# Moving half of the loads of filter taps from ScalarE's queue to GpSimd's, spreading the other half between loads of x, and reordering the filter steps of a graph network kernel

## The chip, the cores and the metric

The kernel runs on one core of one Trainium2 chip. The metric is the device time of one execution in microseconds (us), median of the runs. Executions of one kernel agree within a few tenths of a per cent here (0.6% at most, in e6_stores_scalar); every run that is compared below is in the fast state. The profiler's span of a run is some 2 us shorter than the time of the same run.

## The reference

The input x is (64, 256, 256): 64 graphs of 256 nodes with 256 channels. What matters is the convolution with 17 taps:

```python
h = relu(layernorm(x))                          # per node
xc = transpose(h, (0, 2, 1))
c = relu(bn1(conv1d(xc, conv1_w, pad=0)))       # 256x256, one tap
c = bn2(conv1d(c, conv2_w, pad=8))              # 256x256, 17 taps
x_conv = transpose(relu(c + xc), (0, 2, 1))
# ... messages over exp(-dist) * adj, then a GRU cell of x_conv, messages and h
return x + gru(...)
```

All is float32.

## The kernel before

The 17-tap convolution is done with transforms of 16 bins, so in the opening the kernel must turn `conv2_w` (the *taps*, 4.4 MB) into filters at the transform's points. This is one small matmul per group of 7 input channels, pass and half: 3 passes times 19 groups = 57 *filter steps*. Each step makes a PSUM tile, ScalarE copies it to an `fo` buffer, and a DMA stores it to a tensor in DRAM, from which the products of the batches load weights `wb`.

```python
KG = P // TAPS                  # 7 channels a group: 7 * 17 = 119 partitions
NG = -(-P // KG)                # 19 groups
taps = stage.tile([KG * TAPS, NG, DC, D], FP, name="taps")

def load_taps(dc, a, b, eng):   # dc: which half of the input channels
    eng.dma_start(out=taps[:, a:b, dc, :],
                  in_=c2_wT[dc * P + a * KG:dc * P + b * KG].rearrange("(g k) t o -> (k t) g o", k=KG))
...                             # (the points of the three passes, on ScalarE's queue)
for h in range(3):
    for dc in range(DC):
        load_taps(dc, h * (NG - 1) // 3, (h + 1) * (NG - 1) // 3, nc.scalar if dc else nc.sync)
for dc in range(DC):            # the rows of the last, smaller group
    last = c2_wT[dc * P + (NG - 1) * KG:(dc + 1) * P]
    nc.sync.dma_start(out=taps[:last.shape[0] * TAPS, NG - 1, dc, :], in_=last.rearrange("k t o -> (k t) o"))
...
def transpose_h(i):             # TensorE transposes x, ScalarE copies to HT
    for dc in range(DC):
        p = aux()
        ...
        nc.scalar.activation(HT[i][:, dc, :], p, AF.Relu)
    if i + 2 < B // G:
        load_x(i + 2, nc.scalar if i < 2 else nc.sync)
...
def filters(m, g, eng):         # one filter step
    p = acc()                   # five PSUM buffers
    for dc in range(DC):
        mm(...)                 # points[m] x taps[:, g, dc]
    t = stage.tile([P, W], FP, name="fo", bufs=6)
    nc.scalar.copy(t[:size * kinds], p[:size * kinds])
    eng.dma_start(out=filt[m][...], in_=t[:size * kinds])
```

The schedule of the opening has four *rounds* (transposes of x, conv1, four filter steps) and then the other filter steps. In their midst the first nine `wb` loads are issued on SyncE's queue:

```python
steps = [(m, g) for m in range(len(PASSES)) for g in range(NG)]
transpose_h(0)
norm(1)
w_msg = ...                     # loads of w_msg and the first adj on SyncE's queue
load_adj(0, nc.sync)
for j in range(PB):             # four rounds
    if j > 0: transpose_h(j)
    if 0 < j < PB - 1: norm(j + 1)
    conv1(j)
    run(split_steps(j))
    for m, n in steps[j * 4:(j + 1) * 4]:
        filters(m, n, nc.sync)
...
for j, (m, n) in enumerate(steps[PB * 4:]):
    filters(m, n, nc.gpsimd if j % 2 else nc.sync)
    if j + PB * 4 == 2 * NG - 10:
        for n in range(3):
            for kind in range(3):
                load_kind(0, n, kind)
```

An engine's program runs in order: what stands behind a waiting instruction or a DMA that can't yet be issued waits too. ScalarE's first copy, for example, stood behind 16.48 us of issuing here, though its input was done at 12.87 us.

Of the kernel before, what the change touches and what calls it, by code (L numbers as in the profile page):

```python
# [13 lines left out]
FP = mybir.dt.float32  # L14
U16 = mybir.dt.uint16
AF = mybir.ActivationFunctionType
# [264 lines left out]
def filter_points(bins, taps):  # L281


    cols = []
    for n in bins:
        z = [(ROOTS[n] if n < 15 else 1.0) ** (taps - 1 - t) for t in range(taps)]
        if n < 15:
            cols += [[v.real for v in z], [v.imag - v.real for v in z], [v.real + v.imag for v in z]]
        else:
            cols += [[1.0] * taps, [(-1.0) ** (taps - 1 - t) for t in range(taps)]]  # L290
    return np.array(cols, np.float64).T
# [10 lines left out]
def kernel(  # L302
# [26 lines left out]
    nc = tc.nc  # L329
    P = 128  # L330
    B, N, D = x.shape
    G = 2
    GB = 8
    PB = GB // G
    NB = B // GB
    DC = D // P
    MC = N // P
    W = G * N
    TAPS = c2_wT.shape[1]
# [9 lines left out]
    const = ctx.enter_context(tc.tile_pool(name="const", bufs=1))  # L349
    work = ctx.enter_context(tc.tile_pool(name="work", bufs=1))  # L350
    stage_ctx = ExitStack()
    stage = stage_ctx.enter_context(tc.tile_pool(name="stage", bufs=1))
# [16 lines left out]
    def chunk(t, g, c):  # L369
        return t[:, g * N + c * P:g * N + (c + 1) * P]  # L370
# [4 lines left out]
    def load_rows(t, src, i, eng):  # L375
        for g in range(G):
            eng.dma_start(out=row_tile(t, g), in_=rows(src, G * i + g))

    def load_x(i, eng=nc.sync):
        X[i] = work.tile([P, G * MC, D], FP, name="x", bufs=2)  # L380
        load_rows(X[i], x, i, eng)
# [23 lines left out]
    def load_adj(i, eng=nc.gpsimd):  # L405
        if i >= B // G:
            return
        if i < BY_DMA:
            ADJ[i] = work.tile([P, G * MC, N], FP, name="adj")
            load_rows(ADJ[i], adj, i, eng)  # L410
            return
        ADJH[i] = late.tile([P, 2 * MC, W], U16, name="adjh")
        for q in range(2 * MC):
            eng.dma_start(out=ADJH[i][:, q], in_=ADJD[i][:, q])
# [26 lines left out]
    neg_half = const.tile([P, G * MC], FP)  # L441
    nc.gpsimd.memset(neg_half, -0.5)

    pace = Pace()

    def mm(p, w, v, columns, **kw):
# [3 lines left out]
    def transpose(p, v):  # L450
        nc.tensor.transpose(p, v, ident)  # L451
        pace.tensor(P / 2)
# [6 lines left out]
    def norm_steps(i):  # L459

        if i >= B // G:
            return [], []
        t = {}

        def stats(j):
            if j == 0:
                t["st"] = work.tile([P, G * MC, 6], FP, name="st")
                t["mv"] = work.tile([P, G * MC, 2], FP, name="mv")
                t["rstd"] = work.tile([P, G * MC], FP, name="rstd")
            nc.vector.bn_stats(t["st"][:, j, :], X[i][:, j, :])  # L470

        def aggregate_stats():
            for j in range(G * MC):
                nc.vector.bn_aggr(t["mv"][:, j, :], t["st"][:, j, :])
            nc.vector.tensor_scalar(t["rstd"], t["mv"][:, :, 1], LN_EPS, None, ALU.add)  # L475
            nc.gpsimd.tensor_tensor(t["rstd"], t["rstd"], neg_half, ALU.pow)  # L476

        def scale(j):
            nc.vector.tensor_scalar(X[i][:, j, :], X[i][:, j, :], t["mv"][:, j, 0:1], t["rstd"][:, j:j + 1],
                                    ALU.subtract, ALU.mult)  # L480

        R = range(G * MC)
        return ([(D, lambda j=j: stats(j)) for j in R] + [(W, aggregate_stats)],
                [(D, lambda j=j: scale(j)) for j in R])

    def run(steps):
        for n, call in steps:
            pace.vector(n)
            call()

    def norm(i):
        a, b = norm_steps(i)
        run(a)
        pace.vector(0, pace.dve + 1.4)
        run(b)
# [3 lines left out]
    def vec(src, name, eng=nc.gpsimd):  # L499
        k = src.shape[0] // P  # L500
        t = const.tile([P, k], FP, name=name)
        eng.dma_start(out=t, in_=src.rearrange("(k p) -> p k", p=P))
        return t

    def bn_vecs(params, name, eng=nc.gpsimd):
        return [vec(a, f"{name}_{s}", eng) for a, s in zip(params, "gbmv")]

    def fold_bn(params, name, factor=1.0):
        g, b, m, v = params
        scale = const.tile([P, DC], FP, name=f"{name}_scale")  # L510
        shift = const.tile([P, DC], FP, name=f"{name}_shift")
        nc.vector.tensor_scalar(scale, v, BN_EPS, None, ALU.add)
        nc.gpsimd.tensor_tensor(scale, scale, neg_half[:, :DC], ALU.pow)
        nc.vector.tensor_mul(scale, scale, g)
        nc.vector.tensor_mul(shift, m, scale)
        nc.vector.tensor_sub(shift, b, shift)
        if factor != 1.0:
            nc.vector.tensor_scalar(scale, scale, factor, None, ALU.mult)
        return scale, shift

    w_c1 = const.tile([P, DC, D], FP)
    nc.scalar.dma_start(out=w_c1, in_=c1_wT.rearrange("(k p) o -> p k o", p=P))
    s1, h1_shift = fold_bn(bn_vecs(bn1, "bn1", nc.scalar), "bn1")


    KG = P // TAPS
    NG = -(-P // KG)
    taps = stage.tile([KG * TAPS, NG, DC, D], FP, name="taps")

    def load_taps(dc, a, b, eng):  # L530
        eng.dma_start(out=taps[:, a:b, dc, :],
                      in_=c2_wT[dc * P + a * KG:dc * P + b * KG].rearrange("(g k) t o -> (k t) g o", k=KG))

    PASSES = [range(0, 6), range(6, 12), range(12, 16)]
    points = []
    for n, bins in enumerate(PASSES):
        f = filter_points(bins, TAPS)
        m = np.zeros((KG, TAPS, KG, f.shape[1]), np.float32)
        for k in range(KG):
            m[k, :, k] = f  # L540
        t = stage.tile([KG * TAPS, KG * f.shape[1]], FP, name=f"points{n}")
        nc.scalar.dma_start(out=t, in_=nc.inline_tensor(m.reshape(KG * TAPS, -1), name=f"points{n}").ap())
        points.append(t)
    for h in range(3):
        for dc in range(DC):
            load_taps(dc, h * (NG - 1) // 3, (h + 1) * (NG - 1) // 3, nc.scalar if dc else nc.sync)
    for dc in range(DC):
        last = c2_wT[dc * P + (NG - 1) * KG:(dc + 1) * P]
        nc.sync.dma_start(out=taps[:last.shape[0] * TAPS, NG - 1, dc, :], in_=last.rearrange("k t o -> (k t) o"))


    Z = const.tile([P, 1 + MC, G * MC, Q], FP, name="z")
# [12 lines left out]
    def aux():  # L565
        return psum.tile([P, W], FP, name="aux", bufs=3)
# [5 lines left out]
    def transpose_h(i):  # L572
        if i >= B // G:
            return
        HT[i] = work.tile([P, DC, W], FP, name="hT", bufs=6)
        for dc in range(DC):
            p = aux()
            for j in range(G * MC):
                transpose(chunk(p, j // MC, j % MC), X[i][:, j, dc * P:(dc + 1) * P])
            nc.scalar.activation(HT[i][:, dc, :], p, AF.Relu)  # L580
        if i + 2 < B // G:
            load_x(i + 2, nc.scalar if i < 2 else nc.sync)



# [44 lines left out]
    def load_kind(b, n, kind):  # L630
        b, n = b + n // BINS, n % BINS
        if b < NB and (n < BINS - 1 or kind < 2):
            WB[b, n, kind] = work.tile([P, DC, D], FP, name="wb", bufs=9)
            m = n // len(PASSES[0])
            nc.sync.dma_start(out=WB[b, n, kind], in_=filt[m][:, 3 * (n - PASSES[m][0]) + kind])
# [209 lines left out]

    w_ih = const.tile([P, 2 * DC, 3 * D], FP)
    w_hh = const.tile([P, DC, 3 * D], FP)
    steps = [(m, g) for m in range(len(PASSES)) for g in range(NG)]
    transpose_h(0)
    norm(1)  # L850

    w_msg = const.tile([P, DC, D + SE], FP)
    nc.sync.dma_start(out=w_msg[:, :, :D], in_=msg_wT.rearrange("(k p) o -> p k o", p=P))
    nc.gpsimd.dma_start(out=w_msg[:, :, D:], in_=se_wT.rearrange("(k p) s -> p k s", p=P))
    b_msg = const.tile([P, D + SE], FP)
    for t, v in ((b_msg[:, :D], msg_b), (b_msg[:, D:], se_b)):
        nc.gpsimd.dma_start(out=t, in_=bass.AP(tensor=v.tensor, offset=v.offset, ap=[[0, P], [1, v.shape[0]]]))
    load_adj(0, nc.sync)
    bn2 = bn_vecs(bn2, "bn2")
    b_ih, b_hh = vec(ih_b, "b_ih"), vec(hh_b, "b_hh")  # L860
    for j in range(PB):
        if j > 0:
            transpose_h(j)
        if 0 < j < PB - 1:
            norm(j + 1)
        conv1(j)
# [3 lines that stand above are left out]
# [5 lines left out]
    forward()  # L875
    for j, (m, n) in enumerate(steps[PB * 4:]):
        filters(m, n, nc.gpsimd if j % 2 else nc.sync)
        if j + PB * 4 == 2 * NG - 10:
            for n in range(3):
                for kind in range(3):  # L880
                    load_kind(0, n, kind)
# [5 lines left out]
    for b in range(NB):  # L887
        i = b * PB
# [158 lines left out]
```

## Time and profile before

| | before |
|---|---|
| time, median of three runs | 1900.42 us |
| span of the profiled run | 1895.5 us |
| TensorE busy, whole span | 96% |
| TensorE busy, first 111.5 us | 75.8 us |
| first message matmul (end of the opening) | 111.51 us |

The page cuts the span into 40 slices and gives busy shares in tenths. The timeline merges neighbouring instructions of one kind: its columns are the start in us, the length in us, engine, line, operation, output and inputs, count, and in brackets how long the engine was idle before it and what ended that. The lines that carry the argument stand in the prediction.

### The profile page before, as it was taken

Reading aid. Unit: us, or ns where it says so; the run is one execution under the profiler, and the core shown is the slowest. Engines: PE = TensorE matmul, PEld = TensorE weight load, DVE = VectorE, ACT = ScalarE, POOL = GpSimd, SP = SyncE. Lnnn points to the kernel's source line nnn. Section 1 sums busy time; section 2 is a strip of 40 time slices with the busy share of each in tenths; the row PEclk is TensorE's granted clock in tenths of the full one; section 3 lists DMA queues with packets and bytes.
Section 4 is the critical chain, followed back from the end, with each engine's and each line's share of the span. In section 5 each row is a group of like instructions: output and inputs, shape, how many; then the busy total and the mean of one; then the engine's idle time right before and its main releaser. Section 6 shows DMA issues by size and latency. Waiting matters only on the chain.

```text
span 1895.5 us, 21978 instructions
## 1 busy us (share of the span) xinstructions
PE 1827.6 (96%) x7708; PEld 1136.6 (60%) x7708; DVE 1393.1 (73%) x2667; ACT 639.4 (34%) x1338; POOL 208.2 (11%) x324
## 2 busy tenths in 40 slices
PE   3999999999999999999999999999999999999997
PEld 2677445865549554694458755495546944586543
DVE  2888648996499945998379964999559983798522
ACT  1534322243313443244232433134432352224311
POOL 2110110110111010111101001101101111010000
PEclk9999999999999999999999999999999999999999
DMA  5777331762318431482316613274313923073010
GB/s 161 253 237 216 91 87 36 195 176 57 85 48 244 107 93 52 112 239 56 89 34 191 182 54 82 54 237 114 90 55 106 239 62 78 23 186 104 2 43 23
DMA packets 180215, 217.63 MB, mean 115 GB/s; under 512 B 86146, under 2 KB 105858, under 8 KB 180105
## 3 DMA queue, kind: packets, MB, share of 16 engines
q1 hardware_dynamic: 145228, 156.03, 28.8%
q0 software_dynamic: 30432, 56.53, 12.7%
q10 hardware_dynamic: 4445, 3.67, 0.6%
q8 instruction: 61, 1.00, 0.2%
q14 instruction: 49, 0.40, 0.1%
HBM read 156.54 MB, written 44.30 MB: 106 GB/s over the span
## 4 chain that ended last, share of the span: by engine, by line
PE 82%; DVE 8%; DMA 4%; issue 3%; ACT 2%; POOL 1%; POOLq 0%; DVEq 0%; ACTq 0%
PE acc L447 70%; PE aux L447 8%; PE aux L451 3%; DMA taps<-in_c_wT_dram 1%; DVE Yv L59 1%; PE aux L736 1%; DVE e L743 1%; DVE Yv L62 1%; DMA x<-in_x_dram 1%; DVE T L65 1%; DVE Yv L65 1%; DVE V L65 1%; DMA wb<-filt 1%; DVE msg L708 1%; DVE T L62 0%
## 5 line engine op out<-in xcount | busy, mean ns | idle before, releaser
L447 PE MATMUL acc<-hT,w_hh 128*128 128x512 f32 x768 | 353.9, 597 | 1.9 <-ACT h L593 1.9
L447 PE MATMUL acc<-xnm,w_ih 128*128 128x512 f32 x768 | 353.0, 594 | 0.0
L447 PE MATMUL acc<-Yv,w_ih 128*128 128x512 f32 x768 | 341.1, 593 | 9.5 <-ACT Yv L696 9.5
L447 PEld LDWEIGHTS acc<-Yv,w_ih 128*128 128x128 f32 x768 | 145.2, 190 | 196.3 <-issue 177.2
L447 PEld LDWEIGHTS acc<-xnm,w_ih 128*128 128x128 f32 x768 | 145.6, 190 | 183.3 <-issue 181.3
L447 PEld LDWEIGHTS acc<-hT,w_hh 128*128 128x128 f32 x768 | 143.5, 191 | 169.5 <-issue 161.4
L797 ACT ACTIVATE tr<-acc,b_rz 128x512 f32<-128x512 f32 x64 | 44.0, 687 | 540.8 <-PE acc L447 540.8
L799 DVE SCALAR_TENSOR_TENSOR gn<-tr,gn 128x512 f32<-128x512 f32 x64 | 44.2, 690 | 207.7 <-ACT tr L797 207.7
L825 POOL DMA_DIRECT2D out_dram<-y x64 | 39.2, 617 | 886.4 <-DVE y L824 885.0
L447 PE MATMUL acc<-hT,w_c 128*128 128x512 f32 x256 | 117.9, 604 | 15.2 <-ACT hT L580 15.2
L447 PE MATMUL acc<-U,wb 128*128 128x128 f32 x1024 | 124.6, 276 | 0.5 <-DMA wb<-filt 0.5
L447 PE MATMUL acc<-V,wb 128*128 128x128 f32 x1024 | 124.8, 275 | 0.0
L447 PEld LDWEIGHTS acc<-U,wb 128*128 128x128 f32 x1024 | 120.5, 192 | 4.3 <-DVE Yv L59 2.3
L59 DVE SCALAR_TENSOR_TENSOR V<-T,V 128x256 f32<-128x256 f32 (+2 forms) x224 | 121.5, 606 | 0.3
L447 PEld LDWEIGHTS acc<-V,wb 128*128 128x128 f32 x1024 | 119.5, 192 | 0.0
L447 PE MATMUL aux<-e,msg 128*128 128x256 f32 x464 | 104.9, 379 | 0.0
L447 PEld LDWEIGHTS aux<-e,msg 128*128 128x128 f32 x464 | 86.1, 190 | 11.4 <-issue 1.0
L476 POOL TENSOR_TENSOR rstd<-rstd,neg_half 128x4 f32<-128x4 f32 x32 | 36.3, 1135 | 502.0 <-DVE rstd L475 502.0
L824 DVE TENSOR_TENSOR y<-aux,y 128x512 f32<-128x512 f32 x64 | 41.1, 683 | 68.4 <-PE aux L451 68.4
L447 PE MATMUL aux<-w_msg,hT 128*128 128x259 f32 x384 | 89.4, 381 | 0.0
L65 DVE TENSOR_TENSOR V<-h 128x512 f32<-128x512 f32 x64 | 43.8, 684 | 60.8 <-ACT h L593 60.8
L447 PEld LDWEIGHTS acc<-hT,w_c 128*128 128x128 f32 x256 | 49.2, 194 | 65.2 <-issue 45.1
(141 smaller groups left out, 2727.6 us busy)
## 6 DMA issues: line engine op xcount, KB each, us to landing
wb<-filt SPq DMA_DIRECT2D x376, 256.0 KB
y<-in_x_dram POOLq DMA_DIRECT2D x64, 256.0 KB, 5.7
out_dram<-y POOLq DMA_DIRECT2D x64, 256.0 KB, 5.1
x<-in_x_dram SPq DMA_DIRECT2D x60, 256.0 KB
halves_d<-halves SPq DMA_DIRECT2D x116, 128.0 KB
adjh<-halves_d POOLq DMA_DIRECT2D x116, 128.0 KB, 5.5
filt<-fo SPq DMA_DIRECT2D x26, 252.0 KB
filt<-fo POOLq DMA_DIRECT2D x10, 252.0 KB, 5.6
```

Of the source, the lines that this page charges most:

```text
L59: return self.step(out, lambda: self.v.scalar_tensor_tensor(out, x, s, y, op0=ALU.mult, op1=ALU.add))
L62: return self.step(out, lambda: self.v.tensor_add(out, x, y))
L65: return self.step(out, lambda: self.v.tensor_sub(out, x, y))
L447: nc.tensor.matmul(p, w, v, **kw)
L451: nc.tensor.transpose(p, v, ident)
L476: nc.gpsimd.tensor_tensor(t["rstd"], t["rstd"], neg_half, ALU.pow)
L708: nc.vector.tensor_add(MSG[i][:, g, c, :], p[:, :D + SE], b_msg)
L736: nc.tensor.matmul(p[:, :N], ZT[rows_q, :P], ZT[rows_q, P:], start=True, stop=True)
L797: nc.scalar.activation(tr, pr, AF.Tanh, bias=b_rz[:, dc:dc + 1], scale=0.5)
L799: nc.vector.scalar_tensor_tensor(gn, tr, 1.0, gn, op0=ALU.add, op1=ALU.mult)
L824: nc.vector.tensor_add(row_tile(Y[i], g), p, row_tile(Y[i], g))
L825: nc.gpsimd.dma_start(out=rows(out, G * i + g), in_=row_tile(Y[i], g))
```

## The change

The intent: ScalarE shall not issue loads of taps, so that it can copy the first transposes at once. GpSimd gets the loads of one half of the channels (all of them at the start), SyncE those of the other in thirds, each behind a load of x. Filter steps now take the first third of the groups through all passes first, so that few taps are needed early. A dummy activation loads ScalarE's table before it is needed. The first `wb` loads move from step 28 to step 40.

```diff
+    def load_last_taps(dc, eng):
+        last = c2_wT[dc * P + (NG - 1) * KG:(dc + 1) * P]
+        eng.dma_start(out=taps[:last.shape[0] * TAPS, NG - 1, dc, :], in_=last.rearrange("k t o -> (k t) o"))
+    THIRDS = [(h * (NG - 1) // 3, (h + 1) * (NG - 1) // 3) for h in range(3)]
+    load_taps(0, *THIRDS[0], nc.sync)          # ahead of norm(0)
+    for t in THIRDS:
+        load_taps(1, *t, nc.gpsimd)
+    load_last_taps(1, nc.gpsimd)
...
+    nc.scalar.activation(const.tile([P, 1], FP, name="unused"), neg_half[:, :1], AF.Relu)
...
-    for h in range(3):
-        for dc in range(DC):
-            load_taps(dc, h * (NG - 1) // 3, (h + 1) * (NG - 1) // 3, nc.scalar if dc else nc.sync)
-    (and the last rows of both halves on nc.sync)
...
-            load_x(i + 2, nc.scalar if i < 2 else nc.sync)
+            load_x(i + 2)
...
-    steps = [(m, g) for m in range(len(PASSES)) for g in range(NG)]
+    FIRST = THIRDS[0][1]
+    steps = [(m, g) for g in range(FIRST) for m in range(len(PASSES))]
+    steps += [(m, g) for m in range(len(PASSES)) for g in range(FIRST, NG)]
     transpose_h(0)
+    load_taps(0, *THIRDS[1], nc.sync)
...                                            # in round j == 1, behind the third load of x:
+            load_taps(0, *THIRDS[2], nc.sync)
+            load_last_taps(0, nc.sync)
+            nc.sync.dma_start(out=w_msg[:, :, :D], ...)
+            load_adj(0, nc.sync)
...
-        if j + PB * 4 == 2 * NG - 10:
+        if (m, n) == (1, NG - 4):
```

More of the change, by code (lines that the diff above doesn't have):

```diff
@@ L442, with load_taps @@
     nc.gpsimd.memset(neg_half, -0.5)
+    KG = P // TAPS
+    NG = -(-P // KG)
+    taps = stage.tile([KG * TAPS, NG, DC, D], FP, name="taps")
+    def load_taps(dc, a, b, eng):
+        eng.dma_start(out=taps[:, a:b, dc, :],
+                      in_=c2_wT[dc * P + a * KG:dc * P + b * KG].rearrange("(g k) t o -> (k t) g o", k=KG))
+    def load_last_taps(dc, eng):
[6 more added lines that the diff above has]
+    load_last_taps(1, nc.gpsimd)
     pace = Pace()
@@ L522 @@
     nc.scalar.dma_start(out=w_c1, in_=c1_wT.rearrange("(k p) o -> p k o", p=P))
-    s1, h1_shift = fold_bn(bn_vecs(bn1, "bn1", nc.scalar), "bn1")
-    KG = P // TAPS
-    NG = -(-P // KG)
-    taps = stage.tile([KG * TAPS, NG, DC, D], FP, name="taps")
-    def load_taps(dc, a, b, eng):
-        eng.dma_start(out=taps[:, a:b, dc, :],
-                      in_=c2_wT[dc * P + a * KG:dc * P + b * KG].rearrange("(g k) t o -> (k t) g o", k=KG))
+    bn1 = bn_vecs(bn1, "bn1", nc.scalar)
+    nc.scalar.activation(const.tile([P, 1], FP, name="unused"), neg_half[:, :1], AF.Relu)
+    s1, h1_shift = fold_bn(bn1, "bn1")
     PASSES = [range(0, 6), range(6, 12), range(12, 16)]
@@ L543 @@
         points.append(t)
-    for h in range(3):
-        for dc in range(DC):
-            load_taps(dc, h * (NG - 1) // 3, (h + 1) * (NG - 1) // 3, nc.scalar if dc else nc.sync)
-    for dc in range(DC):
-        last = c2_wT[dc * P + (NG - 1) * KG:(dc + 1) * P]
-        nc.sync.dma_start(out=taps[:last.shape[0] * TAPS, NG - 1, dc, :], in_=last.rearrange("k t o -> (k t) o"))
     Z = const.tile([P, 1 + MC, G * MC, Q], FP, name="z")
@@ L847 @@
     w_hh = const.tile([P, DC, 3 * D], FP)
-    steps = [(m, g) for m in range(len(PASSES)) for g in range(NG)]
+    FIRST = THIRDS[0][1]
+    steps = [(m, g) for g in range(FIRST) for m in range(len(PASSES))]
+    steps += [(m, g) for m in range(len(PASSES)) for g in range(FIRST, NG)]
     transpose_h(0)
+    load_taps(0, *THIRDS[1], nc.sync)
     norm(1)
     w_msg = const.tile([P, DC, D + SE], FP)
-    nc.sync.dma_start(out=w_msg[:, :, :D], in_=msg_wT.rearrange("(k p) o -> p k o", p=P))
     nc.gpsimd.dma_start(out=w_msg[:, :, D:], in_=se_wT.rearrange("(k p) s -> p k s", p=P))
@@ L857 @@
         nc.gpsimd.dma_start(out=t, in_=bass.AP(tensor=v.tensor, offset=v.offset, ap=[[0, P], [1, v.shape[0]]]))
-    load_adj(0, nc.sync)
     bn2 = bn_vecs(bn2, "bn2")
@@ L863 @@
             transpose_h(j)
+        if j == 1:
+            load_taps(0, *THIRDS[2], nc.sync)
+            load_last_taps(0, nc.sync)
+            nc.sync.dma_start(out=w_msg[:, :, :D], in_=msg_wT.rearrange("(k p) o -> p k o", p=P))
+            load_adj(0, nc.sync)
         if 0 < j < PB - 1:
```

## The prediction

> **What bounds the kernel now.** I read the page first: busy shares, the 40 slices, the chain that ended last. TensorE is busy 96% of the 1895.5 us span, and the first slice and a half are the only poor ones, so I then read the opening stage alone: stretches of time with their busy sums, the timeline of the first 115 us by engine, and who waited for whom.
>
> ```profile
> PE   3999999999999999999999999999999999999997
> PEld 2677445865549554694458755495546944586543
> DVE  2888648996499945998379964999559983798522
> ...
> DMA  5777331762318431482316613274313923073010
> ```
>
> The reader sees TensorE ("PE") below 90% only in slice 1 (0 to 47 us) and the last. The stretches confirm it: TensorE was busy 75.8 of the first 111.5 us, 198.0 of the next 200 us from 200 on, and 1469.1 of the last 1495. After 111.5 us (the first message matmul) the kernel is bound by TensorE; what can be won by rearranging loads is in the first 111.5 us. There, the timeline of TensorE alone (start, length, group, count, idle before):
>
> ```profile
> 10.57 2.30 PE L451 MATMUL aux<-ident,x 128*128 128x128 f32 x8 [10.57 <-DVE x L479]
> 27.48 5.38 PE L447 MATMUL acc<-hT,w_c 128*128 128x512 f32 x8 [14.61 <-ACT hT L580]
> 32.69 2.76 PE L447 MATMUL acc<-taps,points 119*126 119x256 f32 x12
> 39.45 2.07 PE L447 MATMUL acc<-taps,points 119*126 119x256 f32 x4 [4.00 <-ACT h L593]
> ...
> 64.94 25.79 PE L447 MATMUL acc<-taps,points 119*126 119x256 f32 x116
> 93.89 2.25 PE L447 MATMUL acc<-taps,points 119*77 119x256 f32 x8 [3.17 <-ACT fo L623]
> ```
>
> and the timeline of ScalarE:
>
> ```profile
> 9.02 16.48 ACTq L531 DMA_DIRECT2D taps<-in_c_wT_dram  x3
> 25.53 1.28 ACT L580 ACT_TABLE_LOAD   x1 [25.53 <-DMA taps<-in_c_wT_dram]
> 26.82 1.08 ACT L580 ACTIVATE hT<-aux 128x512 f32<-128x512 f32 x2
> 35.84 2.64 ACTq L377 DMA_DIRECT2D x<-in_x_dram  x2
> 38.61 1.45 ACT L593 ACTIVATE h<-acc,bn_shift,bn_scale 128x512 f32<-128x512 f32 x2 [10.70 <-DMA taps<-in_c_wT_dram]
> ```
>
> These are three holes. The transposes of the first x are done at 12.87 us, but ScalarE, which must copy them out, issues three loads of taps until 25.50, then loads its table, so conv1 starts at 27.48: 14.6 us lost. A load of x queued behind the taps on ScalarE holds the next h until 38.61: 4 us lost and TensorE cools down. At 90.7 to 100.9 us, TensorE stops for the copies to `fo`, which wait for stores of filters (the waits of ScalarE for `filt<-fo` sum to 18.3 us).
>
> **What the Trainium skill says.** "DMA: Bandwidth & Descriptors", section "Why a DMA increments its semaphore by 16 and not by 1": a DMA from SyncE's or ScalarE's queue uses the largest k up to 16 that divides the slowest dimensions; 119 partitions give k = 7, while some of GpSimd's copies take 16. The trace agrees as far as it can: while mostly taps flow, about half of the DMA engines are busy, and the rate is low.
>
> ```profile
> 14.00:16.00 2.00, 0.00 (x0) 0.00 (x0) 0.84 (x7) 0.00 (x0) 1.20 (x2) 1.00 0.48 149
> 26.00:28.00 2.00, 0.53 (x1) 0.50 (x2) 0.00 (x0) 1.90 (x3) 0.00 (x0) 1.00 0.49 159
> 42.00:44.00 2.00, 2.00 (x7) 1.32 (x6) 0.58 (x1) 1.34 (x3) 0.00 (x0) 0.50 0.47 163
> 48.00:50.00 2.00, 2.00 (x11) 1.75 (x10) 1.20 (x7) 1.88 (x4) 0.49 (x1) 1.00 0.90 320
> ```
>
> The last two columns are DMA share and GB/s. The same page, "Issuing engines are not separate DMA queues", says that issuing from several engines saves only the sequencer's time, usually small; here that time is 16.48 us of ScalarE, so not small. "ScalarE: Activation LUTs", section "What ACT_TABLE_LOAD costs", gives some 1283 ns; the trace has 1.28 us. "TensorE: Matmul & The Clock Gate", Part 1, says that TensorE runs at half clock after some 3.4 us of idleness until it has been busy as long; the clock column reads 0.50 from 38 to 44 us, after the 36-to-39 hole. Agreed.
>
> **The change part by part.** The order of instructions built from both kernels shows that VectorE's order is the same, and TensorE's differs only in which filters are made when. ScalarE loses its three tap loads and two x loads from the opening and has its table load ahead of the first copy. SyncE gets taps for the first half of the channels in thirds, each behind a load of x; GpSimd gets the other half at about 1.4 us.
>
> 1. *First hole.* Transposes end at 12.87; the first copy takes 0.6 us (the later ones' 0.60), so conv1 could start about 13.2 instead of 27.48: saves **14.3 us**, including the 1.28 us of the table.
> 2. *Second hole.* From 32.69 the first four filter steps (16 matmul records) should take the 3.62 us of the later rounds, not 8.6: saves **5.0 us**. The second round of transposes, conv1 and filters took 9.74 us, part of it at half clock, later ones 8.97 (51.05 to 60.02): **0.7 us**. TensorE still starts cold once; no change.
> 3. *Third hole.* From 64.94 there are 41 steps. At 25.79/116 us per record, 164 records are 36.5 us; they took 46.6 (to 111.51): **10.1 us** of waiting. Its cause: six `fo` buffers against stores of 252 KB each, while nine weight loads for the first products (from 81.9, 6.97 us of SyncE's issue time) share the queue and the DMA is at 99% from about 82 to 98 us. The change moves this trigger from step 28 of 57 to step 40, so 8 of SyncE's stores lie behind the nine loads instead of 14, and spreads the smaller stores of pass three. But everything starts earlier against the same bytes: some 23 MB (208 GB/s by 111.5 us). By 90 us that needs 23/90 = 256 GB/s as a mean, though the first 20 us will hardly exceed 180, so about 280 in the rest; the busiest 2 us had 320 and the best slices near 400. It fits, barely. I choose to keep two thirds of this hole: **3.5 us** saved.
> 4. *Cost: contention for the first x.* The tap loads of GpSimd (2.2 MB) now run from about 2.5 us beside x. x's halves landed at 6.21 and 7.63 us in a DMA at 0.54; sharing should delay them by about 1 us: **-1 us**. GpSimd spends four issues (a 0.8 us issue was `w_ih`'s, which I take as size) before 6 us, so its first power at 9.03 isn't held.
> 5. *Cost: taps and x just in time.* Taps landed in before by about 46 us: 7.4 MB in 44 us = 168 GB/s. With 2.2 MB spread over more DMA engines, the first third must be there by 20 us, x2 by 30, x3 by 40. SyncE's `fo` stores of rounds two and three stand behind 0.7 MB of taps, w_msg and adj; with six buffers, round three can hang on them: **-1.5 us** together.
>
> Sum: 14.3 + 5.0 + 0.7 + 3.5 - 1 - 1.5 = **21.0 us**, all on the path since TensorE is the bound afterwards and keeps the lead. VectorE keeps up: its forward transform (34.4 us from 70.2 to 104.6) starts 17.5 us earlier, and it idled 6.9 us for the first message, so it is just ready. It would cap the saving at about 25.
>
> **The rivals.**
> *A: the DMA becomes the bound of the opening.* For: 99% share at 82 to 98 us, and the same bytes in less time; the third hole then grows by what the others give up. Against: share of 0.62 at 60 to 70, and 0.5 up to 46. It would leave a saving of 10 to 13 us: 1888 to 1890.
> *B: GpSimd blocks.* If its four tap loads (714 runs of 1 KB each) take several us each or wait for room, the power of the first norm, then x and the transposes, start late by 5 to 10 us: 1885 to 1890. Against: 0.5 to 0.9 us for every other issue on GpSimd.
> *C: VectorE becomes the bound early in the first batch,* so that time won in the third hole is lost there: saving 20 at most even if the stores run freely.
> *D: all holes close:* 14.3 + 5.0 + 0.7 + 10.1 = 30 us less about 2: 1872. The change can do no more.
>
> **Range and chances.** 1900.4 - 21 = **1879.4 us**. Rival D with VectorE's cap gives 1872, A or B 1889: range **1871.5 to 1889**. Faster by over 2% would need under 1862.4, 38 us, more than all idle time of the opening (111.5 - 75.8 = 35.7, of which 10.6 are the wait for the first x and stay): 1%. Slower by 2% has nothing that speaks for it: under 1%. Within 2%: 98.5%.
>
> **What would show it right or wrong.** conv1's first matmul at 13 to 15 us (step 1); no wait of 4 us for h in the first filters and no 0.50 clock around 40 us (step 2); the first message matmul near 90 us instead of 111.5, with a hole of 4 to 9 us for `fo` left (step 3); the first statistics at 7 to 9 us instead of 6.2 (step 4); waits for taps or x in rounds two to four under 3 us in sum (step 5). From the first message on, both kernels should need the same time within 2 us: 1784 us to the end. If that stretch is longer, C or a DMA backlog carried into the first products is the reason; if GpSimd's issues last to 9 us or longer, B. It is wrong if the taps by GpSimd arrive late and the filters wait for them, or if the stores take up the whole of what the start wins.

## The result, and the profile after

The changed kernel took **1902.72 us** (median of four runs, 1901.48 to 1904.51) and the kernel before **1900.29 us** (four runs). The ratio is 1.0015 with a 95% interval of 0.9997 to 1.0032: the same time. All ratios here are the mean time of one kernel's fast runs over that of the other's of the same rounds, so not quite the ratio of the medians. The profiled run of the changed kernel is the slowest of its four (1904.51 us, span 1902.7); that of the kernel before took 1897.25 us. So spans differ by 7.2 us and medians by 2.4, and only differences of several us in the opening are read from the traces.

TensorE's timeline of the changed kernel:

```profile
11.77 2.30 PE L472 MATMUL aux<-ident,x 128*128 128x128 f32 x8 [11.77 <-DVE x L500]
13.90 5.26 PE L468 MATMUL acc<-hT,w_c 128*128 128x512 f32 x8
36.74 5.79 PE L468 MATMUL acc<-taps,points 119*126 119x256 f32 x16 [17.59 <-DMA taps<-in_c_wT_dram]
...
64.03 5.40 PE L468 MATMUL acc<-hT,w_c 128*128 128x512 f32 x8 [3.93 <-ACT hT L587]
69.27 33.56 PE L468 MATMUL acc<-taps,points 119*126 119x256 f32 x152
103.23 3.14 PE L468 MATMUL acc<-taps,points 119*77 119x256 f32 x12 [0.41 <-ACT fo L630]
...
116.08 4.54 PE L468 MATMUL aux<-w_msg,hT 128*128 128x259 f32 x12
```

conv1 starts at 13.90 us instead of 27.48, as foreseen. Then TensorE waits 17.59 us for taps: the first filter runs at 36.74 us, **4.05 us later than before** (32.69). The hole has not gone, it has moved behind conv1. A new hole of 3.93 us precedes the fourth conv1, and the end of the opening is at 116.08 us instead of 111.51. ScalarE's timeline:

```profile
4.22 1.28 ACT L545 ACT_TABLE_LOAD   x1 [4.22 <-issue]
...
13.25 0.60 ACT L587 ACTIVATE hT<-aux 128x512 f32<-128x512 f32 x1 [7.53 <-PE aux L472]
...
26.35 1.45 ACT L600 ACTIVATE h<-acc,bn_shift,bn_scale 128x512 f32<-128x512 f32 x2 [11.66 <-POOL h L566]
...
62.37 1.12 ACT L630 COPY fo<-acc 126x512 f32<-126x512 f32 x2 [4.24 <-DMA filt<-fo]
```

The table and the first copy come early. But even `h` comes at 26.35 us: bn1's variance, one of the small loads on ScalarE's queue, lets VectorE start at 23.79 (11.40 before). That does no harm beside the 36.74 us. The wait of 4.24 us for an `fo` buffer is the cause of the hole ahead of the fourth conv1, since ScalarE copies `hT` in order behind it: it ended at 62.37 us, and the copies of `hT` ran at 63.39.

Which queue got what, from 12 to 18 us? The DMA view of a window gives each queue's packets, megabytes and packet time as a share of 16 engines (q0: GpSimd, q1: SyncE, q10: ScalarE). The kernel before:

```profile
q1 hardware_dynamic: 516, 0.52, 28.3%
q10 hardware_dynamic: 501, 0.36, 20.1%
q0 software_dynamic: 18, 0.00, 0.9%
```

and the changed kernel:

```profile
q0 software_dynamic: 338, 0.78, 84.7%
q1 hardware_dynamic: 80, 0.16, 18.4%
q10 hardware_dynamic: 151, 0.00, 4.0%
```

The sum is 0.89 MB before and 0.94 MB after, nearly the same rate. But now GpSimd's queue has five sixths of it, taps of all its thirds at once, two of which aren't needed until much later, and SyncE's queue, with the second x and its first third, has 0.16 MB. Packet by packet, the trace says how: GpSimd's taps go in packets of 4096 bytes, SyncE's x in packets of 2048 and its taps in packets of 1024. The first third on SyncE's queue (714 packets of 1024 bytes) begins only at 21.8 us: 123 packets start from 18 to 24 us, 263 from 24 to 30, and the rest by 37.

Stretches of the changed kernel that answer to those in the prediction (stretch, length, busy us of TensorE, its weight loads, VectorE, ScalarE and GpSimd with counts, TensorE's clock, DMA share, GB/s):

```profile
14.00:16.00 2.00, 2.00 (x4) 0.97 (x4) 0.00 (x0) 0.60 (x1) 0.00 (x0) 1.00 1.06 151
26.00:28.00 2.00, 0.00 (x0) 0.00 (x0) 1.09 (x7) 1.45 (x2) 1.12 (x2) 0.50 0.49 132
```

A DMA share of 1.06 with 151 GB/s is no sign of more data moved: more packets are under way at once, and each takes longer. One of 4096 bytes on GpSimd's queue took 0.42 us on average from 6 to 12 us; in the first run below, where only GpSimd's first third is under way then, it took 0.19. The clock of 0.50 shows TensorE cooled by the wait.

**The third hole.** From the fourth conv1 on, 45 filter steps remain (57 less the 12 of three rounds), in 180 records. They took 46.6 us before (64.94 to 111.51) and 46.8 after (69.27 to 116.08). The prediction, and the expectations below, count 41 steps and 36.5 us without waits; that is a miscount, since the merged row from 64.94 on holds the fourth round's four steps too. Runs below that have no hole take 39.6 to 39.7 us for the 45 steps, so the hole was 6.9 us before and is 7.1 after. Where an expectation says "41 steps", read the stretch from the fourth conv1 to the first message.

### The profile page after: what moved, and what is told of

It is laid out like the page before. It is cut to its first block, busy times and chain, and to the rows that moved or that the text cites. A ratio compares the mean times of both kernels' runs of the same rounds, so it can differ in the third digit from the quotient of the medians.

```text
span 1902.7 us, 21985 instructions
## 1 busy us (share of the span) xinstructions
PE 1833.7 (96%) x7708; PEld 1139.4 (60%) x7708; DVE 1393.6 (73%) x2667; ACT 640.5 (34%) x1339; POOL 212.4 (11%) x328
## 4 chain that ended last, share of the span: by engine, by line
PE 82%; DVE 8%; DMA 4%; issue 3%; ACT 1%; POOL 1%; POOLq 0%; SPq 0%; DVEq 0%; ACTq 0%
PE acc L468 70%; PE aux L468 8%; PE aux L472 3%; DMA taps<-in_c_wT_dram 2%; DVE Yv L59 1%; PE aux L743 1%; DVE e L750 1%; DVE Yv L62 1%; DMA x<-in_x_dram 1%; DVE T L65 1%; DVE Yv L65 1%; DMA wb<-filt 1%; DMA filt<-fo 1%; DVE msg L715 1%; DVE V L65 1%
## 5 line engine op out<-in xcount | busy, mean ns | idle before, releaser
L468 PEld LDWEIGHTS aux<-w_msg,hT 128*128 128x128 f32 x384 | 72.8, 193 | 14.9 <-issue 4.7
```

The source lines that it names most:

```text
L468: nc.tensor.matmul(p, w, v, **kw)
```

## The experiments

Fourteen kernels, all correct, all run beside the kernel before.

**1. Which of the first wait's two suspects: turns between queues, or too few DMA engines?** Four runs. The first issues only GpSimd's first third at the start:

```diff
-    for t in THIRDS:
-        load_taps(1, *t, nc.gpsimd)
-    load_last_taps(1, nc.gpsimd)
+    load_taps(1, *THIRDS[0], nc.gpsimd)
...  (behind GpSimd's small loads)
+    load_taps(1, *THIRDS[1], nc.gpsimd)
+    load_taps(1, *THIRDS[2], nc.gpsimd)
+    load_last_taps(1, nc.gpsimd)
```

> The changed kernel, but GpSimd issues only its first third of the taps at the start; its other two thirds and the last rows follow after its small loads, at some 20 us. Theory T1 (GpSimd's taps, in 4 KB packets, take turns with SyncE's 1 and 2 KB packets and hold back the second x and SyncE's first third): the second x lands by 14 us, SyncE's first third by 22 us, the first filter runs at 20 to 24 us instead of 36.7, and the time falls by 8 to 15 us to 1888 to 1895. Rival T2 (all taps go over too few DMA engines, whatever the order): the first filter stays later than 30 us and the time within 3 us of the changed kernel's.

Measured: 1897.48 us, ratio to before 0.9995 (0.998 to 1.001). TensorE:

```profile
23.36 5.34 PE L466 MATMUL acc<-taps,points 119*126 119x256 f32 x16 [4.19 <-DMA taps<-in_c_wT_dram]
...
57.22 5.47 PE L466 MATMUL acc<-hT,w_c 128*128 128x512 f32 x8 [7.14 <-ACT hT L585]
```

The first filter came at 23.36 us instead of 36.74 with nothing but GpSimd's *later* thirds held back. So those thirds, not the first ones, kept SyncE's queue from delivering; this part of T1 is shown. SyncE's queue got 0.57 MB from 12 to 18 us instead of 0.16. That the time fell by 5 us only (3.8 by the two ratios to the kernel before) and not by 8 to 15, so that the range of 1888 to 1895 was missed, has its reason in what follows. The fourth x came late (its second half at 45.45 us, a wait of 2.93 us ahead of its transposes), and the wait for `fo` buffers ahead of the fourth conv1, the second line, grew from 3.93 to 7.14 us.

The second run cuts each load of taps at partition 112, since 112 is a multiple of 16 and 119 is 7 times 17:

```diff
-        eng.dma_start(out=taps[:, a:b, dc, :], in_=...)
+        src = c2_wT[...].rearrange("(g k) t o -> (k t) g o", k=KG)
+        for r in (slice(0, 112), slice(112, KG * TAPS)):
+            eng.dma_start(out=taps[r, a:b, dc, :], in_=src[r])
```

(and the 34 last rows at 32). The rule that the expectation means is the one that the prediction cites, of "DMA: Bandwidth & Descriptors", section "Why a DMA increments its semaphore by 16 and not by 1".

> The changed kernel, but each load of taps is cut into partitions 0 to 111 and 112 to 118 (and 32 and 2 of the last rows), so that by the Trainium skill's rule the large part takes 16 DMA engines instead of 7; who issues what and when is unchanged. T2 (too few engines): the rate in 6 to 30 us rises from 150 to over 250 GB/s, the first filter runs at 18 to 24 us, the time falls by 10 to 18 us. T1 (turn-taking between the queues alone): the rate stays near 150 GB/s and the first filter later than 28 us.

Measured: **1886.86 us**, ratio 0.9949 (0.9932 to 0.9965). The rate from 6 to 18 us rose from 157 to 161 GB/s to 222 to 234, less than the 250 expected, and the first filter ran at 25.44 us, later than the 18 to 24 expected:

```profile
25.44 3.69 PE L471 MATMUL acc<-taps,points 119*126 119x256 f32 x16 [1.82 <-DMA taps<-in_c_wT_dram]
```

The effect of the cut is shown: the same bytes in the same queues and order land much sooner. That it comes of more DMA engines, as T2 has it, is shown only in part. Which engine a packet took, the trace doesn't tell, but its records tell how many packets of a queue were under way at once. Where GpSimd's first third runs alone on its queue (the first run, 6 to 15 us) there were never more than 8 packets of taps; with the cut (e5_late_sixteen) up to 15. But in the changed kernel GpSimd's loads run side by side: from 6 to 12 us their packets took 72.3% of 16 engines' time, so 11.6 were under way on average, and with the cut 78.5%, or 12.6. What fell there is the time of a packet of 4096 bytes, from 0.42 to 0.28 us; why, no run shows. Either edit alone takes 11 to 13 us from the first filter's start.

The cut has a cost that the taps hid: ScalarE's three loads of `points` took 7.95 us to issue (2.83 without the cut), so its first copies came at 17.02 us only, after a wait of 3.42 us for TensorE.

The third run issues all taps on SyncE's queue, both halves of a third in a row.

```diff
-    for t in THIRDS:
-        load_taps(1, *t, nc.gpsimd)
-    load_last_taps(1, nc.gpsimd)
+    for dc in range(DC):          # and likewise for the second and third thirds
+        load_taps(dc, *THIRDS[0], nc.sync)
```

> The changed kernel, but no taps on GpSimd's queue: SyncE issues both halves of each third in the places where it issued one. T1: x lands undisturbed as in the kernel before (second half at 7.6 us, second x by 13 us), both first thirds by 24 us, first filter at 22 to 26 us, the time falls by 6 to 12 us to 1890 to 1896. If one queue alone is slow (some 75 GB/s, what each of two queues had in the kernel before), the first thirds land at 13 + 19 = 32 us, and the time stays within 4 us of the changed kernel's.

Measured: 1902.97 us, ratio 1.0026. The first matmuls of a filter ran at 18.24 us, the others after a wait at 24.38, as T1 says. The time did not fall by the 6 to 12 us expected: the stores of filters now stand behind the taps of both halves on one queue (those of the second round were issued from 51.25 us on, the last taps until 48.45), and the fourth conv1 waited 13.10 us for `fo` buffers.

```profile
24.38 6.19 PE L466 MATMUL acc<-taps,points 119*126 119x256 f32 x14 [5.54 <-DMA taps<-in_c_wT_dram]
...
61.77 6.70 PE L466 MATMUL acc<-hT,w_c 128*128 128x512 f32 x8 [13.10 <-ACT hT L585]
```

The fourth run takes from the kernel before only ScalarE's issuing:

```diff
-    load_taps(dc, ..., nc.scalar if dc else nc.sync)
+    load_taps(dc, ..., nc.sync)
...
-            load_x(i + 2, nc.scalar if i < 2 else nc.sync)
+            load_x(i + 2)
```

> The kernel before, with ScalarE's loads of taps and of x moved to SyncE's queue and nothing else. conv1 starts at 14 to 15 us instead of 27.5. If the opening is bound by ScalarE's issuing (the prediction's first step), the time falls by 10 us or more. If the taps' delivery bounds it, the first filter runs no earlier than 22 us, the third x lands later than 45 us behind all taps, and the time stays within 4 us of the kernel before.

Measured: 1901.58 us, ratio 1.0017 (1.0003 to 1.0032). conv1 ran at 12.98 us; then

```profile
24.20 6.08 PE L447 MATMUL acc<-taps,points 119*126 119x256 f32 x14 [5.49 <-DMA taps<-in_c_wT_dram]
...
52.89 2.29 PE L451 MATMUL aux<-ident,x 128*128 128x128 f32 x8 [14.29 <-DVE x L479]
```

Removing the first hole's visible cause in this way gains nothing: ScalarE's 16 us of issuing lay above a delivery of taps and x that is hardly faster. The first filters did come 8.5 us earlier; what they won went in the third round, whose x this run issues behind all the taps on one queue, at 39.07 us (35.84 on ScalarE's queue before). No run moves the taps and leaves x where it was, so how much of the hole was to be had in another order is open. This queue alone moved 988 KB in the 7 us from 30 to 37 us (141 GB/s), so a single queue isn't slow as such. With 119 partitions a load, 6 to 11 of its packets were under way at once, 7.7 on average.

**2. Do the two edits add, and what is the wait for `fo`?** Both edits together:

> Both edits together on the changed kernel: GpSimd's second and third thirds late, and every load of taps cut at partition 112. If holding back SyncE's queue and too few engines are two separate causes of the late first filter, the first filter runs at 17 to 20 us (25.4 with the cut alone, 23.4 with the late issue alone) and the time is 4 to 9 us under the 1886.9 us of the cut alone. If they are one cause, the first filter stays at 23 us or later and the time within 2 us of the cut alone.

Measured: 1891.54 us, ratio 0.9962 (0.9943 to 0.9981): by the medians 4.7 us above the cut alone, but that ran in another call, and by the ratios it is 2.5 us with intervals that overlap. So it is no better, and not shown to be slower. The filter at 21.97 us needed no wait for taps any more; its start was set by the first x, whose second half came at 12.09 us. Neither of the two forecasts held. What was won went at the fourth conv1, which waited 7.60 us for `hT`; the late thirds now run from 30 to 44 us (1.49 MB on GpSimd's queue), beside the stores.

The first 16 stores on ScalarE's queue:

```diff
-            filters(m, n, nc.sync)
+            filters(m, n, nc.scalar)
```

> As the run before it in this call, and the first 16 stores of filters are issued on ScalarE's queue, so they do not stand behind the last thirds of taps, w_msg and adj on SyncE's. If that order on SyncE's queue makes the 3 to 4 us wait ahead of the fourth conv1 (ScalarE waiting for a free fo buffer), that wait goes, and the time falls by 3 to 6 us. Rival: the stores then wait for the same DMA engines, or ScalarE loses as much to issuing (16 issues of some 0.6 us), and the time stays within 2 us.

Measured: 1895.59 us, but with a spread of 1890.67 to 1901.45; ratio 0.999 (0.9965 to 1.0015). It is no better: the wait went to the third round (10.82 us ahead of its conv1). Inconclusive as to its reason.

The nine `wb` loads behind the last filter:

```diff
-        if (m, n) == (1, NG - 4):
-            (nine load_kind calls)
+    (the same nine calls behind the loop)
```

> As the first run of this call, but the nine weight loads of the first products are issued after the last filter's store instead of in the midst of the filters. If the nine loads cause the third hole (41 filter steps take 46 us where TensorE needs 36.5), the 41 steps fall to 37 to 40 us, though the first products may then wait up to 8 us for their weights. If the stores themselves fill the DMA, the 41 steps still take more than 43 us.

Measured: 1886.24 us, ratio 0.9931 (0.9914 to 0.9948), 5.3 us under the run with both edits. The stretch of 45 steps fell from 47.1 to 40.1 us, so the nine loads have a part in the third hole. The first products then waited 2.2 us for weights.

Eight `fo` buffers:

```diff
-        t = stage.tile([P, W], FP, name="fo", bufs=6)
+        t = stage.tile([P, W], FP, name="fo", bufs=8)
```

> As the first run of this call, with eight fo buffers instead of six (what fits). If the third hole comes of the latency of stores against too few buffers, the 41 steps fall by 2 us or more, and the wait ahead of the fourth conv1 goes. If the stores' throughput bounds it, two buffers only put the wait off by two steps: the 41 steps fall by under 2 us.

Measured: **1879.02 us**, ratio 0.9893 (0.9875 to 0.9911), 12.5 us under the same kernel with six.

```profile
46.13 2.29 PE L473 MATMUL aux<-ident,x 128*128 128x128 f32 x8 [3.07 <-DVE x L501]
48.26 5.63 PE L469 MATMUL acc<-hT,w_c 128*128 128x512 f32 x8
53.73 39.71 PE L469 MATMUL acc<-taps,points 119*126 119x256 f32 x180
93.36 2.90 PE L469 MATMUL aux<-w_msg,hT 128*128 128x259 f32 x12
```

All 180 records in one row without a wait: the third hole is gone although the nine loads lie in its midst, and so is the 7.60 us wait. Here the hole was a matter of buffers, not of the DMA's throughput.

**3. Are eight buffers enough by themselves?** The same edit on the kernel before, on the changed kernel, and on the changed kernel with the cut:

> The kernel before with eight fo buffers instead of six, nothing else. If too few buffers make the third hole there too, the 41 last filter steps fall from 46.6 us to 38 to 41 and the time by 5 to 8 us. If the hole is of the nine weight loads or of the stores' throughput, the time stays within 2 us.

Measured: 1897.92 us, ratio 0.999 (0.9975 to 1.0006), no gain clear of noise. The last stretch still took 45.6 us:

```profile
93.39 2.13 PE L447 MATMUL acc<-taps,points 119*77 119x256 f32 x8 [0.16 <-ACT fo L623]
98.62 11.52 PE L447 MATMUL acc<-taps,points 119*77 119x256 f32 x44 [3.10 <-ACT fo L623]
```

In the old order of steps 14 of SyncE's stores stand behind the nine `wb` loads; in the new one it is 8. The new order with eight buffers has next to no hole, the old one with eight has. That fits the reason which the prediction gave for moving the trigger; no run moves the trigger alone, so it isn't shown by itself.

> The changed kernel with eight fo buffers, nothing else. If the change lost its gain to the late first filter alone, this stays as far from the kernel before with eight buffers as the changed kernel is from the kernel before (3 to 7 us slower in the opening). If buffers hid part of it, the wait ahead of the fourth conv1 (3.9 us and a half clock after it) goes and the time falls by 9 to 13 us, to 1890 to 1894. The first filter still runs at 36 to 37 us in both.

Measured: 1892.49 us, ratio 0.9958 (0.9938 to 0.9979). The first filter ran at 36.37 us, so the first wait is untouched. The wait ahead of the fourth conv1 went (0.29 us), and the stretch took 40.4 us. So too few buffers, apart from the first wait, account for 10.2 us of the changed kernel's time (10.8 by the ratios). With eight buffers on both sides, the change is worth 5.4 us (1897.92 to 1892.49), late taps and all.

> The changed kernel with the taps' loads cut at partition 112 and eight fo buffers; GpSimd issues all its taps at the start. If the late issue on GpSimd did harm with the cut (1891.5 against 1886.9 us), this is 2 to 6 us under the 1879.0 us of the run with all three: 1873 to 1877. If the buffers' gain depends on it, it is 1879 to 1884.

Measured: 1878.86 us, ratio 0.9889 (0.9871 to 0.9908), level with the run that has the late thirds as well. So with eight buffers the late issue did neither harm nor good.

One step further, w_msg and the first adj behind the first 16 stores:

```diff
-            nc.sync.dma_start(out=w_msg[:, :, :D], ...)      # in round j == 1
-            load_adj(0, nc.sync)
+    nc.sync.dma_start(out=w_msg[:, :, :D], ...)              # behind the four rounds
+    load_adj(0, nc.sync)
```

> As the run before it in this call, with w_msg and the first adj loaded on SyncE's queue behind the first 16 stores instead of among them. If loads on SyncE's queue ahead of the stores hold up the rounds, the wait ahead of the fourth round goes and the time falls by 1 to 4 us. Rival: those loads are needed only at the first message and the same bytes then collide with later stores, so the time stays within 1.5 us.

Measured: 1878.32 us, ratio 0.9884 (0.9868 to 0.9901), not told apart from the run before it, as the rival says. This is the fastest median of all:

```profile
14.85 2.30 PE L475 MATMUL aux<-ident,x 128*128 128x128 f32 x8 [14.85 <-DVE x L503]
18.10 5.27 PE L471 MATMUL acc<-hT,w_c 128*128 128x512 f32 x8 [0.96 <-ACT hT L590]
24.89 3.69 PE L471 MATMUL acc<-taps,points 119*126 119x256 f32 x16 [1.52 <-DMA taps<-in_c_wT_dram]
...
49.95 39.71 PE L471 MATMUL acc<-taps,points 119*126 119x256 f32 x180
89.59 2.90 PE L471 MATMUL aux<-w_msg,hT 128*128 128x259 f32 x12
```

From its first message to its end are 1784.1 us (89.59 to 1873.7), against 1784.0 in the kernel before: the gain of the opening is kept whole.

**4. The first x, and the last combination.**

> As e12_adj_after, but GpSimd issues its taps after the first norm's power instead of ahead of it. If GpSimd's loads delay the first x, the first transposes run at 10.5 to 11 us instead of 14.9, the first filter at 20 to 24 us instead of 24.9, and the time falls by 1 to 5 us to 1873 to 1877. If the taps just come later by what x comes earlier, the first filter stays at 24 to 26 us and the time within 1.5 us.

The edit moves GpSimd's tap loads from before the first norm to behind its power. Measured: 1879.4 us, ratio 0.9901, no gain. The first transposes came at 10.82 us and the first filter at 18.95 (the rest at 21.42). But the third round's transposes now waited 2.83 us for x, and TensorE stood at 91.02 us at the message, against 89.59. GpSimd's loads do delay the first x, by 4 us with the loads cut; what comes earlier at the front comes later at the next x.

> The changed kernel with GpSimd's second and third thirds late and eight fo buffers, without the cut of the loads. If the late issue alone frees SyncE's queue, the first filter runs at 23 to 24 us as with six buffers, the wait ahead of the fourth conv1 goes or shrinks, and the time is 1880 to 1886, between the changed kernel with eight buffers (1892.5) and the cut with eight buffers (1878.9). If the late thirds then collide with the stores, it is 1888 or more.

Measured: 1887.62 us, ratio 0.995 (0.9929 to 0.997), with the first filter at 22.72 us. This is above the range that supposed the late issue suffices, and just under the one for a collision; the last stretch took 41.9 us, with a wait of 1.70 us for `fo`.

The eight combinations of the three edits on the changed kernel, medians in us:

| GpSimd's later thirds | six `fo` | eight `fo` | six `fo`, cut at 112 | eight `fo`, cut at 112 |
|---|---|---|---|---|
| at the start | 1902.72 | 1892.49 | 1886.86 | 1878.86 |
| late | 1897.48 | 1887.62 | 1891.54 | 1879.02 |

The kernel before had medians of 1897.94 to 1900.29, so differences of 2 us between columns aren't to be read.

## Why the prediction was wrong, point by point

The prediction was 1879.4 us with a range of 1871.5 to 1889; measured were 1902.72. It foresaw the class ("within 2%") but missed the time by 23 us. That runs e11_sixteen_fo8 and e12_adj_after come to 1878.9 and 1878.3 us, the predicted time, is luck: they need two or three more edits, their first filter runs at 25 to 26 us, and the whole third hole is closed instead of a part.

- **Step 1, the first hole (14.3 us).** Its cause was read rightly: conv1 came at 13.90 us. Its worth was not. The step took the wait that ended last for the whole bound. Run e4_scalar_free shows that, with ScalarE free and all these loads on one queue, taps are there at 24.20 us and the third x so late that TensorE reaches the third round at 52.89 us, later than before. Of two things that lay over one another only the upper was seen.
- **Step 5, taps just in time (-1.5 us): this is the step that failed.** The first third was to be there "by 20 us", at a cost of 1.5 us for all of the step, and came at 36.7. The wait was 17.59 us, and the first filter 4.05 us later than before. Two assumptions stood behind it. One was that GpSimd's 2.2 MB spread over more DMA engines and so come faster. A single load of 119 partitions had at most 8 packets under way (e1_pool_late); all loads together had 11.6 on average from 6 to 12 us, but each packet took longer: the rate from 6 to 18 us was 157 to 161 GB/s, hardly above the 148 to 168 of the kernel before, and rose only when the loads were cut. The other was that each queue delivers its own in time; GpSimd's queue took 0.78 of 0.94 MB between 12 and 18 us, and holding its later thirds back freed SyncE's. Either edit alone, late thirds or cut, brings the filter to 23 to 25 us.
- **Step 2, the second hole (5.7 us).** The load of x no longer holds ScalarE, and rounds two and three took 8.3 to 8.4 us instead of 9.7 and 9.0: 2.0 us gained from the second transposes to the fourth, more than the 0.7 foreseen. But the first filters ran at half clock because of the new wait (5.79 us, not 3.62; 8.62 before), so they gained 2.8 us of the 5.0.
- **Step 3, the third hole (3.5 us of 10.1).** Mis-sized at both ends. The hole was 6.9 us, by the miscount of steps, and the change saved nothing of it (7.1 us). With six `fo` buffers it stays unless the nine `wb` loads go last (e7_wb_last); with eight it goes in the new order and not in the old. (The DMA share of 99% from 82 to 98 us, on which the step and rival A lean, is that of the busiest part; the mean is 96%.)
- **Step 5 again, `fo` stores behind loads.** The mechanism was right: ScalarE waited 4.24 us for a store and the fourth conv1 3.93 us, and it cost half clock for that conv1 (5.40 against 3.70 us). The size was far below what came of it.
- **Step 4, the first x (-1 us): right.** The second half came at 8.83 instead of 7.63 us, the transposes at 11.77 instead of 10.57. Three of GpSimd's issues took 3.81 us and did not hold its power (rival B fell).
- **Rival A** (the DMA as the bound of the opening) came nearest, but it named the late stretch; the loss lay between 6 and 37 us, at 122 to 161 GB/s, where the cut shows that more was to be had. **Rival C** did not occur; e12_adj_after reaches the first message 21.9 us earlier than the kernel before and needs the same time from there.
- From the message on, both need about the same: 1784.0 and 1786.6 us, the latter with its message matmuls at half clock (4.54 instead of 2.89 us) after the waits before.

Not settled: why the packets of GpSimd's loads, side by side, take twice as long, and why the cut shortens them; how much of the first hole another order of loads could win; and how much of the third hole's end is due to the later trigger alone.

## What to carry to other kernels

When an engine is held by issuing loads, ask before freeing it when the data itself will land; freeing the issuer only moves the wait if the delivery is as late. Loads that are needed late can starve those that are needed first, on whatever queue these are: here holding them back brought the first filter 13.4 us forward. Where a load has an odd partition count such as 119, try a cut at a multiple of 16: here it was worth some 14 us (13.6 to 15.9, by the medians) with GpSimd's loads at the start. After each such edit, look for the next buffer that runs out: here two more `fo` buffers were worth 8 to 12 us once the opening ran closer, and nothing clear before.

## What the Trainium skill lacked or had wrong

- "DMA: Bandwidth & Descriptors", section "Issuing engines are not separate DMA queues", says that issuing from several engines only saves the sequencer's time. That leaves out what the queue decides, who is served first (the page has the turn-taking elsewhere, in the section of the next point): from 12 to 18 us GpSimd's queue moved 0.78 MB and SyncE's 0.16, and the first filter came 13.4 us earlier when GpSimd's later loads were held back. The page calls the sequencer's time usually small; three loads of 714 KB held ScalarE's for 16.48 us, while one such load held SyncE's for 0.32 us in the changed kernel. What sets this time, no run isolates.
- The same page, section "Queues, rings and completion order", gives packets of some 9 to 17 descriptors as typical. In this trace SyncE's rows of 1 KB went in packets of 1024 bytes each, one row a packet. Beside GpSimd's packets of 4096 bytes, and with turns taken by packets as the page says, that is a reason for the unequal shares, though the runs don't isolate it.
- The same page, section "Why a DMA increments its semaphore by 16 and not by 1", says that GpSimd gives some direct copies 16 engines, without saying which. This load of 119 partitions seems not to be one: alone on its queue it had at most 8 packets under way, and up to 15 when cut into 112 and 7. That fits the section's general rule.
- No page says that the profile's DMA share can pass 1: it was 1.06 at 151 GB/s, and 0.96 at 243 GB/s in another run. The share counts overlapping packets' times, so the higher share went with fewer bytes here.
